# A two-layer graph network on one core: maxima with an operand in PSUM, a tile's own rows requested earlier, one slot and one loop test fewer, a square root in the last normalisation

## The chip, the cores and the metric

The kernel runs on one core of a Trainium2 chip. The core has five instruction queues that run side by side and meet through semaphores: TensorE (PE in the profile, its weight loads PEld), VectorE (DVE), ScalarE (ACT), GpSimd (POOL) and SyncE (SP), which issues DMAs. The metric is the device time of one execution in microseconds (us); the kernel before took 4130.41 us (median of 3 runs, 4128.99 to 4130.92).

## What is computed

12500 nodes with 64 features, 200000 edges sorted by destination, two layers. Cut to what matters:

```python
# layer 0
msg = relu(concat([x[dst], x[src], edge_attr, u[dst]]) @ W1 + b1)
agg = segment_sum(msg, dst)
x1  = layernorm(x + relu(concat([x, agg, u]) @ W2 + b2))
# layer 1, 8 relations
Z   = einsum('ni,rio->nro', x1, fc_weight)
e   = relu(sum(concat([Z[src, etype], Z[dst, etype]]) * attn[etype]))
m   = segment_max(e, dst)
a   = exp(e - m[dst]) / segment_sum(exp(e - m[dst]), dst)
out = layernorm(x1 + segment_sum(a * Z[src, etype], dst))
```

Destinations are skewed towards the low nodes (12500 times the square of a uniform number), so a node near the end has about 8 edges and one near the start far more.

## The kernel before

**Edges.** The edges are cut into runs of 512 (four chunks of 128), and two runs make a *group*: 196 groups (`NG`), the last with one run. All destinations of a run lie in a window of 96 nodes; here every run needs one window. A group's source rows are gathered by an indirect DMA per chunk, eight per group, issued by POOL (`gather`, L303; the instruction is L305): in layer 0 from `b_tab`, in layer 1 from `z_tab`, which layer 0 writes.

**Layer 0** (`sum0`, L331): the group's rows of `a_tab`, edge features and relative destinations are loaded by SP, POOL gathers, TensorE forms the messages, VectorE adds, ScalarE clips, TensorE sums by a one-hot matrix `oh` (made at L299 from a row of numbers that lies in PSUM, `psc`), and VectorE adds the sum into `xa`.

**Layer 1** (`sum1`, L527): the same shape of work, with a running maximum. The edge scores `e` are completed at L563 (which needs the gathered rows `zg`) and L564. Then L568 multiplies the one-hot matrix by the scores (128 partitions x 768 elements), and L571 takes the maximum over a run's four chunks in two halvings (384, then 192 elements). TensorE transposes the result (L577), VectorE reduces it (L582), and the maxima, exponentials (L615 to L619) and weighted sums (L623) follow, up to L627 and L628.

**Nodes.** 100 tiles of 125 nodes. A tile can be finished as soon as no later group adds to it. Which tile comes when is worked out from the destinations ahead of layer 0 (L241 to L264): from group 90 (`FIRST`) on there is one *slot* behind each group, and one more behind the last (`LATE`), 107 in all. A slot with nothing new to do repeats a tile; here the one behind the last group is such a slot. `finish0` (L374) loads the tile's own rows of `x` (L382), applies W2, normalises, and writes `x1_tab`, `z_tab` and `d_tab` (L400, L417, L421). `finish1` (L631) loads the tile's rows of `x1_tab` (L638), divides and adds; `scale1` (L652) normalises up to four tiles together and stores them (L670).

**Order.** Inside each layer the order of instructions on every engine is written out by hand. `sum0`, `sum1`, `finish0` and `finish1` are generators, cut by `yield`; each pass of the loop over `i` advances the pieces of groups `i+3` to `i-2` and of some slots. Loads are issued three groups ahead. Buffers are counted per tile (`zg` has five, `bg` and `dw` four).

**Behind each layer** stand loops that a graph with wider runs would need: over further windows (`each_window`, L281) and over tiles left (L515, L742). With these inputs all of them run zero times, but each loop is a test that all engines pass together after the transfers under way have landed.

Of the kernel before, what the change touches and what calls it, by code (L numbers as in the profile page):

```python
# [26 lines left out]
F32 = mybir.dt.float32  # L27
BF16 = mybir.dt.bfloat16
I32 = mybir.dt.int32
# [7 lines left out]
P = 125  # L37
# [14 lines left out]
FIRST = 90  # L52
LATE = 1
NS = NG + LATE
NSL = NS - FIRST
NQ1 = 4
# [6 lines left out]
def gnn_kernel(ctx: ExitStack, tc, x, xT, src, dstp, dst, et, eaT, u, W1, b1, W2, b2, fc, aw, out):  # L63
# [42 lines left out]
    nc.vector.memset(ones_row, 1.0)  # L106
    psc = fixed.tile([128, 512], F32, name="psc")
    nc.vector.tensor_copy(psc[:, :128], iota)
    iota_n, iota_r = psc[:EC, :W], psc[:EC, :NR]
# [31 lines left out]
    count_row = keep.tile([1, NRUN], I32, name="count_row")  # L141
    runs_more = keep.tile([1, 1], I32, name="runs_more")
    slot_row = keep.tile([1, NSL + 1], I32, name="slot_row")

# [23 lines left out]
    with (  # L168
# [71 lines left out]

        lo = [pre.tile([1, 2 * NS], F32, name=f"lo{i}") for i in range(2)]  # L241
        for t in lo:
            nc.vector.memset(t, float(N))
        nc.vector.tensor_reduce(lo[0][:, :NG - 1], both[:, 2, S:].rearrange("o (g s) -> o g s", s=S), AX.X, OP.min)
        step = 1
        while step < NS:
            nc.vector.tensor_tensor(lo[1][:, :NS], lo[0][:, :NS], lo[0][:, step:step + NS], OP.min)
            lo.reverse()
            step *= 2
# [3 lines left out]
        for t in up:  # L253
            nc.vector.memset(t, float(P))
        nc.vector.scalar_tensor_tensor(up[0][:, NSL:], lo[0][:, FIRST:NS], one, paces, OP.mult, OP.subtract)
        step = 1
# [5 lines left out]
        nc.vector.scalar_tensor_tensor(done, up[0][:, NSL:], float(P), paces, OP.min, OP.add)  # L262
        nc.vector.tensor_copy(slot_row[:, NSL:], done[:, NSL - 1:])
        nc.vector.tensor_scalar(slot_row[:, :NSL], done, -float(P), 0.0, OP.add, OP.max)  # L264
        nc.sync.dma_start(base_b, bases[0].partition_broadcast(EC))
# [14 lines left out]

    def each_window(body):  # L281

        last = nc.values_load(runs_more[0:1, 0:1], min_val=0, max_val=NRUN)
        with tc.For_i(0, last) as r:
            n = nc.values_load(count_row[0:1, ds(r, 1)], min_val=1, max_val=NWIN)
            with tc.For_i(1, n) as w:
                body(r, w)

# [85 lines left out]
    def finish0(work, psum, n0_of, dq):  # L374

        n0 = n0_of(ENG.DVE)
        yield
        xs = work.tile([2 * D, P], F32, name="xs")
        nc.vector.tensor_copy(xs, xa[:, ds(n0, P)])
        n0 = n0_of(ENG.SP)  # L380
        xn = work.tile([P, D], F32, name="xn")
        nc.sync.dma_start(xn, x[ds(n0, P), :])  # L382
        yield
# [15 lines left out]
        nc.vector.tensor_scalar(x1, y, mv[:, 0:1], v, OP.subtract, OP.mult)  # L399
        nc.sync.dma_start(x1_tab[ds(n0, P), :], x1)  # L400
        yield
# [15 lines left out]
        nc.sync.dma_start(  # L417
            z_tab[ds(n0 * NR, P * NR), :].rearrange("(p r) c -> p (r c)", r=NR),
            z.rearrange("p r c -> p (r c)"))
        parts(work, pw[:, NR:2 * NR], lambda i: dq[:, i * NR:(i + 1) * NR], [P, NR])  # L420
        nc.sync.dma_start(d_tab[ds(n0, P), :], dq)  # L421

# [36 lines left out]
    def group(g):  # L459
        if 0 <= g < NG:  # L460
            next(groups[g], None)

    def node(i):
        if i in slots:
            next(slots[i], None)

    with (
        tc.tile_pool(name="l0", bufs=2) as work,
        tc.tile_pool(name="l0_ps", bufs=1, space=PSUM) as pool,
        tc.manual_schedule(),  # L470
    ):
        psum = Banks(pool, {"po": "small", "pw": "small"})
        for i in range(-3, NS + 2):
            g = i + 3
            if g < NG:
                n, chunks, c = span(g)
                groups[g] = sum0(work, psum, n, chunks, src_i[:, c], rel[:, c], row_load(work, g),
                                 eaT[g * S:g * S + n], wins_load(g), aws[g % 4])
            if FIRST <= i < NS:
                slots[i] = finish0(work, psum, slot(i), dqs[i % 2])  # L480
            group(i + 3)
            node(i - 2)
            group(i)
            node(i - 1)
            node(i - 2)
            group(i)
            group(i + 2)
            group(i)
            node(i)
            node(i - 1)  # L490
            node(i - 2)
            node(i - 1)
            group(i)
            node(i)
            node(i - 1)
            group(i + 3)
            group(i + 1)
            node(i)

    with (  # L500
# [6 lines left out]

        each_window(more0)

    with (  # L510
        tc.tile_pool(name="r0n", bufs=1) as work,
        tc.tile_pool(name="r0n_ps", bufs=1, space=PSUM) as psum,
    ):
        begin = nc.values_load(slot_row[0:1, NSL:], min_val=0, max_val=N)
        with tc.For_i(begin, N, P) as n0:  # L515
            at = nc.s_assert_within(n0, 0, N - P, skip_runtime_bounds_check_because="the first node of a tile")
            all_of(finish0(work, psum, lambda engine: at, dqs[0]))
    nodes.close()
# [8 lines left out]
    def sum1(work, psum, n, chunks, idx, rel_of, et_of, row_of, wins_of):  # L527
# [38 lines left out]

        oe = work.tile([EC, n, KS, W], F32, name="oe")
        nc.vector.tensor_mul(oe.rearrange("p s i w -> p (s i) w"), oh, e.unsqueeze(2).to_broadcast([EC, n * KS, W]))  # L568
        half = KS // 2
        while half:  # L570
            nc.vector.tensor_max(oe[:, :, :half, :], oe[:, :, :half, :], oe[:, :, half:2 * half, :])  # L571
            half //= 2
        pt = psum.tile([128, n * (EC + W)], F32, name="pt")
        tt = pt[:W, :n * EC].rearrange("p (s e) -> p s e", s=n)
        rows = pt[:C, n * EC:].rearrange("p (s w) -> p s w", s=n)
        for s in range(n):
            nc.tensor.transpose(tt[:, s, :], oe[:, s, 0, :], ident[:EC, :EC])  # L577
        yield
# [51 lines left out]

    def finish1(work, psum, n0_of, y, mv):  # L631

        n0 = n0_of(ENG.Activation)
        own = work.tile([C, P], F32, name="own")
        nc.scalar.copy(own, acc[:, ds(n0, P)])
        n0 = n0_of(ENG.SP)
        xn = work.tile([P, D], F32, name="xn1")
        nc.sync.dma_start(xn, x1_tab[ds(n0, P), :])  # L638
        yield
        pl = psum.tile([P, C], F32, name="pl")  # L640
        nc.tensor.transpose(pl, own, ident[:C, :C])
        yield
        den = work.tile([P, 1], F32, name="den")

# [7 lines left out]
    def scale1(work, n0s_of, y, mv):  # L652
        n = len(n0s_of)

        v = work.tile([P, 2, n], F32, name="ln_v")
        nc.scalar.activation(v[:, 1, :], mv[:, :n, 1], AF.Ln, bias=eps)  # L656
        nc.scalar.activation(v[:, 0, :], v[:, 1, :], AF.Exp, scale=-0.5)
        yield
        nc.vector.tensor_mul(v[:, 1, :], v[:, 0, :], v[:, 0, :])
        again = work.tile([P, n], F32, name="ln_again")  # L660
        nc.vector.scalar_tensor_tensor(again, mv[:, :n, 1], EPS, v[:, 1, :], OP.add, OP.mult)
        nc.vector.tensor_scalar(again, again, -0.5, 1.5, OP.mult, OP.add)
        v = v[:, 0, :]
        nc.vector.tensor_mul(v, v, again)
        shift = work.tile([P, n], F32, name="ln_shift")
# [6 lines left out]
    with (  # L672
# [6 lines left out]

        for i in range(-3, NS + 4):  # L680
            g = i + 3
            if g < NG:
                n, chunks, c = span(g)
                groups[g] = sum1(work, psum, n, chunks, row_i[:, c], rel[:, c], et_i[:, c],
                                 row_load(work, g), wins_load(g))
            q, at = divmod(i - 2 - FIRST, NQ1)
            if FIRST <= i - 2 < NS:
                if at == 0:
                    ys[q] = (work.tile([P, NQ1, D], F32, name="y1"),
                             work.tile([P, NQ1, nc.vector.BN_AGGR_DIM], F32, name="ln_mv"))  # L690
                y, mv = ys[q]
                slots[i - 2] = finish1(work, psum, slot(i - 2), y[:, at, :], mv[:, at, :])
            group(i + 3)
            group(i)
            group(i - 1)
# [22 lines left out]
            q, at = divmod(i - 3 - FIRST, NQ1)  # L718
            if FIRST <= i - 3 < NS and (at == NQ1 - 1 or i - 3 == NS - 1):
                scales = {q: scale1(work, [slot(j) for j in range(i - 3 - at, i - 2)], *ys[q])}  # L720
                next(scales[q])

    with (
# [10 lines left out]

        each_window(more1)

    with (
        tc.tile_pool(name="r1n", bufs=1) as work,
        tc.tile_pool(name="r1n_ps", bufs=1, space=PSUM) as psum,
    ):  # L740
        begin = nc.values_load(slot_row[0:1, NSL:], min_val=0, max_val=N)
        with tc.For_i(begin, N, P) as n0:  # L742
            at = nc.s_assert_within(n0, 0, N - P, skip_runtime_bounds_check_because="the first node of a tile")
            y = work.tile([P, 1, D], F32, name="y1")
            mv = work.tile([P, 1, nc.vector.BN_AGGR_DIM], F32, name="ln_mv")
            all_of(finish1(work, psum, lambda engine: at, y[:, 0, :], mv[:, 0, :]))
            all_of(scale1(work, [lambda engine: at], y, mv))


# [40 lines left out]
```

## Time and profile before

| | |
|---|---|
| median of 3 runs | 4130.41 us |
| the profiled execution | 4140.92 us, span 4139.1 us, TensorE clock granted 0.572 |
| busy share of the span | PE 72%, PEld 56%, DVE 58%, ACT 35%, POOL 72% |
| first to last gather of layer 0 | 111.87 to 2062.87 us |
| first to last gather of layer 1 | 2104.23 to 4093.27 us |

The span runs from the first to the last instruction of the program; the execution's own time is 1.8 us longer. The profiled execution is 10.5 us above the median of the runs. The profile's page gives busy time by engine, the span in 40 slices, and groups of instructions by line: how many, mean ns of one, and what ended the idle time ahead of them. A line such as "x1563 | 1474.9, 944 | 575.2" is 1563 instructions, 1474.9 us busy, 944 ns each, 575.2 us idle ahead of them. In a timeline the columns are start, duration, engine, line, operation, output and inputs with their shapes, and in brackets the idle time before it and its releaser.

### The profile page before, as it was taken

Reading aid. Unit: us, or ns where it says so; the run is one execution under the profiler, and the core shown is the slowest. Engines: PE = TensorE matmul, PEld = TensorE weight load, DVE = VectorE, ACT = ScalarE, POOL = GpSimd, SP = SyncE. Lnnn points to the kernel's source line nnn. Section 1 sums busy time; section 2 is a strip of 40 time slices with the busy share of each in tenths; the row PEclk is TensorE's granted clock in tenths of the full one; section 3 lists DMA queues with packets and bytes.
Section 4 is the critical chain, followed back from the end, with each engine's and each line's share of the span. In section 5 each row is a group of like instructions: output and inputs, shape, how many; then the busy total and the mean of one; then the engine's idle time right before and its main releaser. Section 6 shows DMA issues by size and latency. Waiting matters only on the chain. (4 is left out here: it accounts for less than half of the span.)

```text
span 4139.1 us, 63111 instructions
## 1 busy us (share of the span) xinstructions
PE 3000.7 (72%) x16309; PEld 2329.7 (56%) x16310; DVE 2409.7 (58%) x7823; ACT 1434.5 (35%) x3697; POOL 3000.2 (72%) x3141
## 2 busy tenths in 40 slices
PE   4666766676999999999946665666666667666664
PEld 4455655565777767777735444454444555544553
DVE  3333333333555555555547666666677777777776
ACT  0000000000111111111155555555556666666665
POOL 1677777777777777777757777777777777777774
PEclk9655555555555565555555556655566555566655
DMA  5222222222333333333311111111112222212221
GB/s 131 53 45 46 45 45 46 45 46 44 74 80 78 77 80 79 78 80 77 72 34 28 29 28 28 29 28 28 28 30 35 35 35 34 36 34 35 35 35 24
DMA packets 317468, 201.76 MB, mean 49 GB/s; under 512 B 239840, under 2 KB 239970, under 8 KB 316746
## 3 DMA queue, kind: packets, MB, share of 16 engines
q0 software_dynamic: 100032, 103.43, 14.5%
q1 hardware_dynamic: 201819, 88.13, 9.1%
q10 hardware_dynamic: 15249, 6.10, 0.6%
q8 instruction: 132, 2.16, 0.2%
q14 instruction: 236, 1.93, 0.2%
HBM read 155.21 MB, written 42.17 MB: 48 GB/s over the span
## 5 line engine op out<-in xcount | busy, mean ns | idle before, releaser
L305 POOL DMA_INDIRECT bg<-b_tab,src_i x1563 | 1474.9, 944 | 575.2 <-issue 443.8
L305 POOL DMA_INDIRECT zg<-z_tab,row_i x1563 | 1512.9, 968 | 517.3 <-issue 396.3
L357 PE MATMUL pa<-oh,msg 128*64 128x96 f32 x3128 | 536.4, 363 | 282.7 <-ACT msg L352 281.9
L352 ACT ACTIVATE msg<-msg 128x512 f32<-128x512 f32 x196 | 123.2, 629 | 1706.8 <-DVE msg L351 1690.2
L347 PEld LDWEIGHTS pm<-aw,cb 128*128 128x128 f32 x3128 | 609.6, 299 | 140.3 <-issue 139.5
L357 PEld LDWEIGHTS pa<-oh,msg 128*64 128x64 f32 x3128 | 479.8, 221 | 303.9 <-ACT msg L352 299.3
L347 PE MATMUL pm<-aw,cb 128*128 128x64 f32 x3128 | 643.8, 391 | 0.0
L623 PE MATMUL pb<-oh,wz 128*65 128x96 f32 x3128 | 548.4, 367 | 16.0 <-ACT wz L619 2.9
L351 DVE TENSOR_TENSOR msg<-pm,bg 128x512 f32<-128x512 f32 x196 | 135.2, 690 | 694.0 <-DMA bg<-b_tab,src_i 580.1
L623 PEld LDWEIGHTS pb<-oh,wz 128*65 128x65 f32 x3128 | 494.3, 227 | 72.8 <-ACT wz L619 72.8
L619 ACT ACTIVATE wz<-zg,wz 128x64 f32<-128x64 f32 x1564 | 394.7, 335 | 6.4
L299 DVE TENSOR_TENSOR oh<-psc,rel 128x768 f32<-128x768 f32 x392 | 370.6, 945 | 9.3 <-DMA d_tab<-dq 6.5
L540 PE MATMUL ps_row<-row,ones_row 1*96 1x512 bf16 x391 | 208.0, 532 | 211.0 <-ACT off L541 200.1
L541 ACT ACTIVATE off<-ps_row,minus_p 96x512 bf16<-96x512 f32 x391 | 266.1, 681 | 263.7 <-PE ps_row L540 263.6
L577 PE MATMUL pt<-ident,oe 128*96 128x128 f32 x391 | 123.0, 417 | 323.0 <-DVE mq L369 323.0
L363 DVE TENSOR_TENSOR xa<-xa,pa 64x96 f32 x391 | 100.9, 258 | 334.7 <-PE pa L357 327.3
L584 PE MATMUL pt<-ident,m 96*65 96x96 f32 x782 | 176.5, 379 | 159.1 <-DVE m L582 159.1
L577 PEld LDWEIGHTS pt<-ident,oe 128*96 128x96 f32 x391 | 50.8, 184 | 416.2 <-issue 392.7
L342 DVE TENSOR_SCALAR cb<-ps_row,iota_p 96x1024 f32<-96x1024 f32 x196 | 246.2, 1256 | 8.8 <-PE ps_row L293 8.8
L584 PEld LDWEIGHTS pt<-ident,m 96*65 96x65 f32 x782 | 119.5, 220 | 176.1 <-DVE m L582 176.1
L293 PE MATMUL ps_row<-row,ones_row 1*96 1x512 bf16 x391 | 199.7, 609 | 17.8 <-DMA row<-rel_tab 16.4
L544 ACT ACTIVATE ohT<-off 96x1024 bf16<-96x1024 bf16 x196 | 206.7, 1054 | 6.3
(139 smaller groups left out, 3581.0 us busy)
## 6 DMA issues: line engine op xcount, KB each, us to landing
z_tab<-z SPq DMA_DIRECT2D x107, 253.9 KB
bg<-b_tab,src_i POOLq DMA_INDIRECT x1563
zg<-z_tab,row_i POOLq DMA_INDIRECT x1563
cb<-in_eaT SPq DMA_DIRECT2D x195, 128.0 KB
aw<-a_tab SPq DMA_DIRECT2D x391, 24.0 KB
dw<-d_tab SPq DMA_DIRECT2D x391, 4.7 KB
row<-rel_tab SPq DMA_DIRECT2D x390, 2.0 KB
xn<-in_x SPq DMA_DIRECT2D x107, 31.2 KB
```

The source lines that it names most:

```text
L293: nc.tensor.matmul(ps[:, s, :RE], ones_row, row[:, s, :], start=True, stop=True)
L299: nc.vector.tensor_tensor(oh, iota_n[:, None, :].to_broadcast([EC, n * KS, W]), rel_of.unsqueeze(2).to_broadcast([EC, n * KS, W]), OP.is_e ...
L305: nc.gpsimd.indirect_dma_start(out=to[:, k, :], out_offset=None, in_=table[:, :], in_offset=bass.IndirectOffsetOnAxis(ap=idx[:, k:k + 1], ...
L342: nc.vector.tensor_scalar(cb[:W, :, :], ps_row, iota_p[:W], None, OP.is_equal)
L347: nc.tensor.matmul(pm[:, k, :], cb[:, s, i * EC:(i + 1) * EC], aw_t[:, s, :], start=True, stop=True)
L357: nc.tensor.matmul(pa[D:, s, :], msg[:, k, :], oh[:, k, :], start=(i == 0), stop=(i == KS - 1))
L540: nc.tensor.matmul(ps_row[:, :RE], ones_row, row[:, s, :], start=True, stop=True)
L541: nc.scalar.activation(off[:, s, :], ps_row[:, :RE], AF.Abs, bias=minus_p[:W])
L544: nc.scalar.activation(ohT, off, AF.Relu, bias=1.0, scale=-1.0)
L584: nc.tensor.matmul(rows[:, s, :], m[:, s:s + 1].to_broadcast([W, C]), ident[:W, :W], start=True, stop=True)
L619: nc.scalar.activation(wz[:, k, :D], zg[:, k, :D], AF.Copy, scale=wz[:, k, D:])
L623: nc.tensor.matmul(sums[:, s, :], wz[:, k, :], oh[:, k, :], start=(i == 0), stop=(i == KS - 1))
```

## The change

- `LATE` goes: no slot behind the last group, 106 slots.
- `finish0` and `finish1` request the tile's own rows in a step of their own, first of all: in layer 0 with the loads of the slot's group, three passes earlier (six buffers); in layer 1 two passes earlier than before (five buffers).
- In `sum1` the product of one-hot matrix and scores is made in two halves, one in SBUF and one in the unused part of the PSUM tile `psc`; three maxima take the place of two, and each has one operand in PSUM.
- Behind each layer one outer loop, run once if tiles are left and not at all otherwise, holds both loops of before.
- `scale1` takes ScalarE's square root and VectorE's reciprocal in place of logarithm, exponential and a Newton step, and calls the exponential on one element behind it.

```diff
-LATE = 1
-NS = NG + LATE
-NSL = NS - FIRST
+NSL = NG - FIRST
...
+        nc.vector.tensor_scalar(rest, done[:, NSL - 1:], float(N), None, OP.is_lt)
...
-    def each_window(body):
-
-        last = nc.values_load(runs_more[0:1, 0:1], min_val=0, max_val=NRUN)
-        with tc.For_i(0, last) as r:
-            n = nc.values_load(count_row[0:1, ds(r, 1)], min_val=1, max_val=NWIN)
-            with tc.For_i(1, n) as w:
-                body(r, w)
+    def leftover(edges, node):
+
+        some = nc.values_load(rest[0:1, 0:1], min_val=0, max_val=1)
+        with tc.For_i(0, some):
+            last = nc.values_load(runs_more[0:1, 0:1], min_val=0, max_val=NRUN)
+            with tc.For_i(0, last) as r:
+                n = nc.values_load(count_row[0:1, ds(r, 1)], min_val=1, max_val=NWIN)
+                with tc.For_i(1, n) as w:
+                    edges(r, w)
+            begin = nc.values_load(slot_row[0:1, NSL:], min_val=0, max_val=N)
+            with tc.For_i(begin, N, P) as n0:
+                node(nc.s_assert_within(n0, 0, N - P, skip_runtime_bounds_check_because="the first node of a tile"))
...
     def finish0(work, psum, n0_of, dq):
 
+        at = n0_of(ENG.SP)
+        xn = work.tile([P, D], F32, name="xn", bufs=6)
+        nc.sync.dma_start(xn, x[ds(at, P), :])
+        yield
         n0 = n0_of(ENG.DVE)
         yield
         xs = work.tile([2 * D, P], F32, name="xs")
         nc.vector.tensor_copy(xs, xa[:, ds(n0, P)])
-        n0 = n0_of(ENG.SP)
-        xn = work.tile([P, D], F32, name="xn")
-        nc.sync.dma_start(xn, x[ds(n0, P), :])
         yield
...
-        for i in range(-3, NS + 2):
+        for i in range(-3, NG + 2):
...
-            if FIRST <= i < NS:
-                slots[i] = finish0(work, psum, slot(i), dqs[i % 2])
+            if FIRST <= g < NG:
+                slots[g] = finish0(work, psum, slot(g), dqs[g % 2])
             group(i + 3)
+            node(i + 3)
             node(i - 2)
...
-        oe = work.tile([EC, n, KS, W], F32, name="oe")
-        nc.vector.tensor_mul(oe.rearrange("p s i w -> p (s i) w"), oh, e.unsqueeze(2).to_broadcast([EC, n * KS, W]))
         half = KS // 2
-        while half:
-            nc.vector.tensor_max(oe[:, :, :half, :], oe[:, :, :half, :], oe[:, :, half:2 * half, :])
-            half //= 2
+        by_run, es = oh.rearrange("p (s i) w -> p s i w", s=n), e.rearrange("p (s i) -> p s i", s=n)
+        oe = work.tile([EC, n, half, W], F32, name="oe")
+        other = psc[:EC, 128:128 + n * half * W].rearrange("p (s i w) -> p s i w", s=n, i=half)
+        for to, i in ((oe, slice(0, half)), (other, slice(half, KS))):
+            nc.vector.tensor_mul(to, by_run[:, :, i, :], es[:, :, i].unsqueeze(3).to_broadcast([EC, n, half, W]))
+        t = work.tile([EC, n, W], F32, name="t")
+        nc.vector.tensor_max(other[:, :, 1, :], oe[:, :, 1, :], other[:, :, 1, :])
+        nc.vector.tensor_max(t, oe[:, :, 0, :], other[:, :, 0, :])
+        nc.vector.tensor_max(t, t, other[:, :, 1, :])
...
-    def finish1(work, psum, n0_of, y, mv):
-
+    def finish1(work, psum, n0_of, y_of):
+
+        n0 = n0_of(ENG.SP)
+        xn = work.tile([P, D], F32, name="xn1", bufs=5)
+        nc.sync.dma_start(xn, x1_tab[ds(n0, P), :])
+        yield
         n0 = n0_of(ENG.Activation)
         own = work.tile([C, P], F32, name="own")
         nc.scalar.copy(own, acc[:, ds(n0, P)])
-        n0 = n0_of(ENG.SP)
-        xn = work.tile([P, D], F32, name="xn1")
-        nc.sync.dma_start(xn, x1_tab[ds(n0, P), :])
         yield
...
-        v = work.tile([P, 2, n], F32, name="ln_v")
-        nc.scalar.activation(v[:, 1, :], mv[:, :n, 1], AF.Ln, bias=eps)
-        nc.scalar.activation(v[:, 0, :], v[:, 1, :], AF.Exp, scale=-0.5)
-        yield
-        nc.vector.tensor_mul(v[:, 1, :], v[:, 0, :], v[:, 0, :])
-        again = work.tile([P, n], F32, name="ln_again")
-        nc.vector.scalar_tensor_tensor(again, mv[:, :n, 1], EPS, v[:, 1, :], OP.add, OP.mult)
-        nc.vector.tensor_scalar(again, again, -0.5, 1.5, OP.mult, OP.add)
-        v = v[:, 0, :]
-        nc.vector.tensor_mul(v, v, again)
+        v = work.tile([P, n], F32, name="ln_v")
+        nc.scalar.activation(v, mv[:, :n, 1], AF.Sqrt, bias=eps)
+        back = work.tile([1, 1], F32, name="back")
+        nc.scalar.activation(back, none[:1], AF.Exp)
+        yield
+        nc.vector.reciprocal(v, v)
...
             group(i + 3)
+            node(i)
             group(i)
```

More of the change, by code (lines that the diff above doesn't have):

```diff
@@ L142, in gnn_kernel @@
     runs_more = keep.tile([1, 1], I32, name="runs_more")
+    rest = keep.tile([1, 1], I32, name="rest")
     slot_row = keep.tile([1, NSL + 1], I32, name="slot_row")
@@ L237, in gnn_kernel @@
         nc.vector.tensor_copy(runs_more, more)
-        lo = [pre.tile([1, 2 * NS], F32, name=f"lo{i}") for i in range(2)]
+        lo = [pre.tile([1, 2 * NG], F32, name=f"lo{i}") for i in range(2)]
         for t in lo:
@@ L245, in gnn_kernel @@
         step = 1
-        while step < NS:
-            nc.vector.tensor_tensor(lo[1][:, :NS], lo[0][:, :NS], lo[0][:, step:step + NS], OP.min)
+        while step < NG:
+            nc.vector.tensor_tensor(lo[1][:, :NG], lo[0][:, :NG], lo[0][:, step:step + NG], OP.min)
             lo.reverse()
@@ L254, in gnn_kernel @@
             nc.vector.memset(t, float(P))
-        nc.vector.scalar_tensor_tensor(up[0][:, NSL:], lo[0][:, FIRST:NS], one, paces, OP.mult, OP.subtract)
+        nc.vector.scalar_tensor_tensor(up[0][:, NSL:], lo[0][:, FIRST:NG], one, paces, OP.mult, OP.subtract)
         step = 1
@@ L399, in finish0 @@
         nc.vector.tensor_scalar(x1, y, mv[:, 0:1], v, OP.subtract, OP.mult)
-        nc.sync.dma_start(x1_tab[ds(n0, P), :], x1)
+        nc.sync.dma_start(x1_tab[ds(at, P), :], x1)
         yield
@@ L417, in finish0 @@
         nc.sync.dma_start(
-            z_tab[ds(n0 * NR, P * NR), :].rearrange("(p r) c -> p (r c)", r=NR),
+            z_tab[ds(at * NR, P * NR), :].rearrange("(p r) c -> p (r c)", r=NR),
             z.rearrange("p r c -> p (r c)"))
         parts(work, pw[:, NR:2 * NR], lambda i: dq[:, i * NR:(i + 1) * NR], [P, NR])
-        nc.sync.dma_start(d_tab[ds(n0, P), :], dq)
+        nc.sync.dma_start(d_tab[ds(at, P), :], dq)
     def slot(i):
@@ L506, in more0 @@
             all_of(sum0(work, psum, 1, KS, idx, rl, lambda: row, eaT[ds(r, 1)], lambda engine: [base], aws[0]))
[L508 to L517, printed above, removed]
+        leftover(more0, lambda at: all_of(finish0(work, psum, lambda engine: at, dqs[0])))
     nodes.close()
@@ L576, in sum1 @@
         for s in range(n):
-            nc.tensor.transpose(tt[:, s, :], oe[:, s, 0, :], ident[:EC, :EC])
+            nc.tensor.transpose(tt[:, s, :], t[:, s, :], ident[:EC, :EC])
         yield
@@ L642, in finish1 @@
         yield
+        y, mv = y_of()
         den = work.tile([P, 1], F32, name="den")
@@ L678, in gnn_kernel, with y_of @@
         groups, slots, ys, scales = {}, {}, {}, {}
-        for i in range(-3, NS + 4):
+        def y_of(i):
+            q, at = divmod(i - FIRST, NQ1)
+            if at == 0:
+                ys[q] = (work.tile([P, NQ1, D], F32, name="y1"),
+                         work.tile([P, NQ1, nc.vector.BN_AGGR_DIM], F32, name="ln_mv"))
+            return ys[q][0][:, at, :], ys[q][1][:, at, :]
+        for i in range(-3, NG + 4):
             g = i + 3
@@ L685, in gnn_kernel @@
                                  row_load(work, g), wins_load(g))
[L686 to L692, printed above, removed]
+            if FIRST <= i < NG:
+                slots[i] = finish1(work, psum, slot(i), lambda i=i: y_of(i))
             group(i + 3)
+            node(i)
             group(i)
@@ L718, in gnn_kernel @@
             q, at = divmod(i - 3 - FIRST, NQ1)
-            if FIRST <= i - 3 < NS and (at == NQ1 - 1 or i - 3 == NS - 1):
+            if FIRST <= i - 3 < NG and (at == NQ1 - 1 or i - 3 == NG - 1):
                 scales = {q: scale1(work, [slot(j) for j in range(i - 3 - at, i - 2)], *ys[q])}
@@ L733, in more1, with node1 @@
             all_of(sum1(work, psum, 1, KS, idx, rl, etx, lambda: row, lambda engine: [base]))
[L735 to L743, printed above, removed]
+        def node1(at):
             y = work.tile([P, 1, D], F32, name="y1")
             mv = work.tile([P, 1, nc.vector.BN_AGGR_DIM], F32, name="ln_mv")
-            all_of(finish1(work, psum, lambda engine: at, y[:, 0, :], mv[:, 0, :]))
+            all_of(finish1(work, psum, lambda engine: at, lambda: (y[:, 0, :], mv[:, 0, :])))
             all_of(scale1(work, [lambda engine: at], y, mv))
+        leftover(more1, node1)
 def kernel(x, src, dst, edge_attr_32, edge_type_8, L0_gnn_u, L0_gnn_W1, L0_gnn_b1, L0_gnn_W2,
```

## The prediction

> **What bounds the kernel now.** I read the page's busy table, then its groups by line, then which engine waited for what, then the timeline of POOL and VectorE side by side, and last the timeline where one layer ends and the next begins.
>
> No engine is over 72% busy on the page, yet one paces both layers. POOL issues 1563 gathers per layer, one after the other:
>
> ```profile
> L305 POOL DMA_INDIRECT bg<-b_tab,src_i x1563 | 1474.9, 944 | 575.2 <-issue 443.8
> L305 POOL DMA_INDIRECT zg<-z_tab,row_i x1563 | 1512.9, 968 | 517.3 <-issue 396.3
> ```
>
> Between two gathers lie 0.30 us of issue, never over 0.32 within a layer. Layer 0's gathers run from 111.87 to 2062.87 us and layer 1's from 2104.23 to 4093.27 us, so the span is 111.9 (preparation) + 1951.0 + 41.4 (seam) + 1989.0 + 45.8 (tail) = 4139.1. TensorE at "9" in the second half of layer 0, VectorE at "7" in layer 1 and every queue wait of SP lie beside POOL's chain. Only two kinds of thing move the end: the time of a gather, and the seam and tail, where POOL has nothing to do.
>
> The two rows differ by 24 ns per gather, 1563 x 0.024 = 37.5 us. In layer 1 every group of eight has seven gathers of 944 ns and one long one. The timeline shows its neighbour:
>
> ```profile
> 3001.28 0.17 DVE L563 TENSOR_TENSOR e<-e,zg 128x8 f32<-128x8 f32 x1 [1.42 <-DMA zg<-z_tab,row_i]
> 3001.68 0.96 DVE L568 TENSOR_TENSOR oe<-oh,e 128x768 f32<-128x768 f32 x1
> 3002.68 0.95 DVE L571 TENSOR_TENSOR oe<-oe 128x384 f32<-128x384 f32 x2
> ```
> ```profile
> 3001.11 0.94 POOL L305 DMA_INDIRECT zg<-z_tab,row_i  x1 [0.30 <-issue]
> 3002.36 1.09 POOL L305 DMA_INDIRECT zg<-z_tab,row_i  x1 [0.30 <-issue]
> 3003.76 0.95 POOL L305 DMA_INDIRECT zg<-z_tab,row_i  x1 [0.30 <-DVE mq L369]
> ```
>
> Over all groups the excess of the long gather is the end of one VectorE instruction, counted from the gather's start, less 127 ns: here L568 ends at 3002.64, 0.28 behind the start, and the excess is 0.15. A gather whose start falls at least 50 ns behind the start of L568 and more than 127 ns ahead of its end is held; one whose start lies anywhere else is not. So a gather needs something for a moment at its start that L568 keeps. Replayed for all groups this gives 37.2 us, the records 37.4. 183 of the 195 long gathers overlap L568 and the replay puts six down to the maxima (L571): the held gather gets through in the 34 ns and the start-up between L568 and L571. L299 of the same size (947 ns, one operand in PSUM) overlaps 380 gathers and lengthens none. The phase is steady because L563 waits for the landing of the group's own last gather: in half the groups L568 starts 593 to 700 ns ahead of the gather that it holds.
>
> The seam's end and the tail's:
>
> ```profile
> 2077.47 0.22 DVE L388 TENSOR_TENSOR y<-po,c 125x64 f32<-125x64 f32 x1 [0.50 <-PE po L385]
> 2078.95 0.33 SPq L382 DMA_DIRECT2D xn<-in_x  x1
> 2081.49 0.22 DVE L389 SCALAR_TENSOR_TENSOR y<-y,xn 125x64 f32<-125x64 f32 x1 [3.79 <-DMA xn<-in_x]
> ...
> 2090.53 0.26 SPq L417 DMA_DIRECT2D z_tab<-z  x1
> ...
> 2095.47 0.26 SPq L421 DMA_DIRECT2D d_tab<-dq  x1
> ...
> 2104.23 0.95 POOL L305 DMA_INDIRECT zg<-z_tab,row_i  x1 [41.17 <-DVE er L555]
> ...
> 4120.37 0.33 SPq L638 DMA_DIRECT2D xn<-x_tab  x1
> 4122.34 0.28 DVE L647 SCALAR_TENSOR_TENSOR y<-pl,den,xn 125x64 f32<-125x64 f32 x1 [6.29 <-DMA xn<-x_tab]
> ```
>
> Slot 195's own rows are requested late and VectorE stands 3.79 us; then slot 196 follows; then two loop tests. In the tail the request of slot 196's rows stands behind four output stores.
>
> **The change: maxima.** The multiply becomes two of 128x384 (558 ns, the one L568 row of that size), both with both inputs in SBUF, the second written to PSUM. They don't depend on each other, and independent neighbours start 80 ns before the predecessor's end (L571 to L369 above), so the second runs from 477 to 1034 ns behind the first's start. The maxima, three of 128x192 (358 ns, L571's row of that size), each have a PSUM operand: like L299 they hold nothing. That relieves those six, 1.3 us. VectorE's work per group goes from 957+34+559+34+358 = 1942 ns to about 2100, and the waits at L563 (mean 1.5 us) hide that; without them L563 would be late by 0.15 us a group, moving the phase.
>
> What matters is the held gather. L568 ended 957 ns behind its start; the second half ends at 1034. The other 184 are held 77 ns longer, 184 x 0.077 = +14.2 us; groups whose multiply starts less than 527 ns ahead of the gather now escape or fall to the shorter first half. Replayed group by group: 43.1 us, +6.
>
> [...] L568's mean is 958 ns and a gather never delays it by more than some 70 ns. [...] by the rows the sum is +6. [...]
>
> No row shows two SBUF inputs with a PSUM output. From below: it holds nothing, only the first half does, and the replay leaves 1.7 us (-36). From above: it holds as L568 and also starts later. I take "holds", as the nearest row is L568, with the same two inputs.
>
> **Seam.** Own rows early: slot 194's wait at L389 (1.22 us) and slot 195's (3.79) go. What is late next is TensorE: z's matmuls of slot 194 end about 2078.4, then the transposition of slot 195 and x1T near 2079.5 instead of 2083.91. From there z takes as long as slot 196's did (x1T 2090.64, z store 2094.96, d_tab store 2095.47), and its store waits for the previous one's landing, so the last z store goes out near 2083.9 instead of 2094.96: -11.1, slot 196's whole step included. Slot 196 only repeats the last tile: worked out from the destinations, the slots up to 195 already reach node 12500, so the loop behind them stays empty. One loop test less: POOL passed the first at 2100.5 and the second at 2102.6: -2.1. Seam -13.2.
>
> **Tail.** VectorE's longer multiply and maxima delay the last two groups by 0.3. The square root leaves two table loads (1.28 us each) per four tiles as before, and two VectorE instructions instead of five (-0.6). The four stores end near 4118.9; they go at 1.74 us each, so those of slots 194 and 195 go near 4120.6 and 4122.4, where the last went at 4130.1: -7.7. The rows of slot 195 have long landed. One test less, SP 4132.0 to 4133.7: -1.9, less rounding. Tail -9.6.
>
> **At nothing.** The requests moved ahead (a register load of 1.7 us and one DMA per slot) pass on SP behind the group's own loads and ahead of stores; SP waits some 700 us in each layer for buffers and loads run three groups ahead, so POOL, which waits only for its own buffers (five), sees nothing. Without that cover each would cost up to 2 us of 10.3 a group. With six and five buffers no request waits for a tile in use. The "rest" instruction, 0.19 us, is hidden behind loads.
>
> Sum on the profiled execution: -13.2 - 9.6 + 6 = -16.8, from its own time of 4140.9 (span 4139.1) to 4124. The median of the runs is 4130.4, 10.5 below the profiled one; the difference carries over: 4113.6, say 4114.
>
> **Rivals.** *PSUM output frees the gather* (0.14): -22.8 - 36 gives 4071. For it: the gap that L299 leaves; against: L299's freedom is that of an input. *Phase* (0.16): if the second half starts 34 ns behind the first's end, as dependent pairs do, and 50 ns later besides, the gather slips through between them in two of three groups: 20 us left, 4130.4 - 22.8 - 17 = 4091. *Slower* (0.06): L563 released some 120 ns later against the gathers, so that the second half starts just ahead of each one's need: held 380 ns, 195 x 0.38 = 74 us, +37 - 23, 4144. It decides from 351 ns a group, where the holds reach 68.4 us and outweigh seam and tail by 0.2%; the seam's savings don't touch it. *It doesn't do what it says* (0.06): the seam waits for stores of z that land no earlier; only the tail's half comes, 4130.4 - 9.6 + 6 = 4127.
>
> **Numbers.** My case has 0.58, with 4100 to 4124 of its own (seam and tail 3 each way, phase). The measurement can tell 0.2%, 8.3 us. Faster: my case, the first two rivals and a little less at the edges, 0.84; same 0.09; slower 0.07. The range takes in the PSUM rival: 4068 to 4124.
>
> **What would show it.** zg's mean gather of 971 ns against 968, one long gather per group of about 1.2 us ending with the second multiply; 945 would mean that PSUM output frees it. First gather of layer 1 about 28 us behind layer 0's last (41.4 before); tail near 36 (45.8). No wait of L389 for xn. Wrong if POOL shows gaps over 0.31 us inside a layer.

## The result, and the profile after

The changed kernel took 4107.67 us (median of 6 runs, 4105.61 to 4110.41), the kernel before 4130.85 us beside it: a ratio of 0.9944, 95% interval 0.9931 to 0.9957, which is 23 us less. The forecast was 4114, 17 us less. The profiled execution of the changed kernel took 4110.41 us, its span 4108.6.

The page of the changed kernel, the gathers of both layers (the columns are as before; the lines of the code have moved, L305 to L311):

```profile
L311 POOL DMA_INDIRECT bg<-b_tab,src_i x1563 | 1475.2, 944 | 574.6 <-issue 435.2
L311 POOL DMA_INDIRECT zg<-z_tab,row_i x1563 | 1507.6, 965 | 501.4 <-issue 423.1
```

POOL still paces both layers, 0.30 us between gathers throughout. But zg's mean is 965 ns, where 971 was expected: the long gathers add up to 32.1 us, less than before (37.4) instead of more. Cut at the first and last gather of each layer, in us:

| | preparation | layer 0 | seam | layer 1 | tail | span |
|---|---|---|---|---|---|---|
| before | 111.9 | 1951.0 | 41.4 | 1989.0 | 45.8 | 4139.1 |
| after | 111.3 | 1951.3 | 25.5 | 1983.7 | 36.9 | 4108.6 |
| forecast | 111.9 | 1951.0 | 28.2 | 1995 | 36.2 | 4122 |

The timelines of VectorE and of POOL around one group of layer 1 in the changed kernel:

```profile
3003.35 0.56 DVE L571 TENSOR_TENSOR oe<-oh,e 128x384 f32<-128x384 f32 x1
3003.83 0.56 DVE L571 TENSOR_TENSOR psc<-oh,e 128x384 f32<-128x384 f32 x1
3004.42 0.36 DVE L573 TENSOR_TENSOR psc<-oe,psc 128x192 f32<-128x192 f32 x1
```
```profile
3002.83 0.94 POOL L311 DMA_INDIRECT zg<-z_tab,row_i  x1 [0.30 <-issue]
3004.08 1.11 POOL L311 DMA_INDIRECT zg<-z_tab,row_i  x1 [0.30 <-DMA zg<-z_tab,row_i]
3005.50 0.94 POOL L311 DMA_INDIRECT zg<-z_tab,row_i  x1 [0.31 <-issue]
```

The two multiplies start 0.48 us apart, as forecast from a neighbour in the kernel before that starts 0.08 us ahead of the end of L571 (3003.63):

```profile
3003.55 0.15 DVE L369 CAST mq<-pb 96x2 bf16<-96x2 f32 x1
```

The second multiply, into PSUM, is the one that runs when the gather at 3004.08 starts. It ends 0.31 us behind that start, and the gather is 0.17 us too long: the end less about 130 ns, the same law that L568 showed before (less 127 ns).

The seam and the tail of the changed kernel, from its timeline:

```profile
2071.86 0.22 DVE L395 TENSOR_TENSOR y<-po,c 125x64 f32<-125x64 f32 x1 [0.27 <-PE po L392]
2072.12 0.22 DVE L396 SCALAR_TENSOR_TENSOR y<-y,xn 125x64 f32<-125x64 f32 x1
...
2079.71 0.26 SPq L424 DMA_DIRECT2D z_tab<-z  x1
2080.21 0.26 SPq L428 DMA_DIRECT2D d_tab<-dq  x1
2085.31 0.23 SPq L444 DMA_DIRECT2D row<-rel_tab  x1
...
2088.06 0.95 POOL L311 DMA_INDIRECT zg<-z_tab,row_i  x1 [25.32 <-issue]
...
4092.08 9.21 SPq L670 DMA_DIRECT2D out<-y  x6
```

L396, which is L389 of before, no longer waits for xn. The last store of z goes out at 2079.71, and six output stores in a row end the work, where four, a request and three more did before.

### The profile page after: what moved, and what is told of

It is laid out like the page before. It is cut to its first block, busy times and chain, and to the rows that moved or that the text cites. A ratio compares the mean times of both kernels' runs of the same rounds, so it can differ in the third digit from the quotient of the medians.

```text
span 4108.6 us, 63192 instructions
## 1 busy us (share of the span) xinstructions
PE 2993.0 (73%) x16301; PEld 2321.8 (57%) x16302; DVE 2440.2 (59%) x8117; ACT 1432.1 (35%) x3693; POOL 2995.2 (73%) x3141
## 5 line engine op out<-in xcount | busy, mean ns | idle before, releaser
L311 POOL DMA_INDIRECT bg<-b_tab,src_i x1563 | 1475.2, 944 | 574.6 <-issue 435.2
L311 POOL DMA_INDIRECT zg<-z_tab,row_i x1563 | 1507.6, 965 | 501.4 <-issue 423.1
L357 DVE TENSOR_TENSOR msg<-pm,bg 128x512 f32<-128x512 f32 x196 | 135.3, 690 | 698.9 <-DMA bg<-b_tab,src_i 553.7
L305 DVE TENSOR_TENSOR oh<-psc,rel 128x768 f32<-128x768 f32 x392 | 370.6, 945 | 12.3 <-DMA row<-rel_tab 9.5
L580 PE MATMUL pt<-ident,t 128*96 128x128 f32 x391 | 123.5, 419 | 326.6 <-DVE mq L375 326.3
L580 PEld LDWEIGHTS pt<-ident,t 128*96 128x96 f32 x391 | 50.8, 184 | 418.6 <-issue 395.1
L299 PE MATMUL ps_row<-row,ones_row 1*96 1x512 bf16 x391 | 197.8, 604 | 17.5 <-DMA row<-rel_tab 16.2
```

The source lines that it names most:

```text
L299: nc.tensor.matmul(ps[:, s, :RE], ones_row, row[:, s, :], start=True, stop=True)
L305: nc.vector.tensor_tensor(oh, iota_n[:, None, :].to_broadcast([EC, n * KS, W]), rel_of.unsqueeze(2).to_broadcast([EC, n * KS, W]), OP.is_e ...
L311: nc.gpsimd.indirect_dma_start(out=to[:, k, :], out_offset=None, in_=table[:, :], in_offset=bass.IndirectOffsetOnAxis(ap=idx[:, k:k + 1], ...
```

## The experiments

The theory, in keeping with L568 (two inputs in SBUF, 183 gathers held) and L299 (one input in PSUM, none held of 380 that overlap it): a gather of layer 1 is held by whichever VectorE instruction with both inputs in SBUF is running as it starts; it ends later by what is left of that instruction at its start, less about 130 ns. Which instruction that is follows from how soon gathered rows land. The gain is in seam and tail. The main rival: the maxima's own reads were the hold and PSUM has relieved them, as the shorter layer 1 suggests.

In what follows *message* is the last group's L351 (L357 in the changed kernel), and *hold* is the sum of what layer 1's gathers last over 944 ns. *Landing* is the time from the start of a group's last gather to the end of VectorE's wait for its rows, median over the early groups of layer 0, where the change alters nothing. Each ratio is to the kernel before, run on the same chip. The kernel before, the maxima alone, everything but the maxima and the multiply freed ran on one chip; the changed kernel, the multiply freed with the maxima in SBUF, the delay and the two loop tests on a second; the slot kept on a third; and three runs, told of last, on a fourth.

**The kernel before, once more**, for a profile beside the others.

> The kernel before, once more, for a profile on the chip of the other runs. Theory (a gather is held until the end of the multiply that runs at its start; how far that is depends on how soon the gathered rows land): if the rows of layer 0 land 2.50 us behind the start of a group's last gather, as in the changed kernel's profile, the long gathers of layer 1 add up to about 28 us and the span is near 4130; if they land at 2.57 us, as in the first profile, to 37 us and 4139. Rival (the landing has no part in it): 37 us whatever the landing.

Landing 2.55 us, hold 38.8, span 4138.9; median 4139.8, ratio 1.0004 (0.9996 to 1.0013). So the rows landed as late as in the first profile (2.57, hold 37.4), and the case of 2.50 us did not come up.

**The maxima alone.**

```diff
-        oe = work.tile([EC, n, KS, W], F32, name="oe")
-        nc.vector.tensor_mul(oe..., oh, e...)
-        while half: ...
+        (the two halves and three maxima of the change)
```

> The kernel before with the halved multiply and the PSUM maxima alone. Theory: the second half ends 77 ns later than the whole multiply did, so layer 1's holds grow by 4 to 6 us and the time with them: 4134 to 4137. Rival (the maxima's SBUF reads held the gathers, PSUM relieves them): layer 1 shorter by 5 us or more, 4126 or less.

Ratio 1.0011 (1.0004 to 1.0018), median 4143.0 against 4138.1: 5 us slower. Hold 41.7 against 38.8 for the kernel before on the same chip (landing 2.56 and 2.55), layer 1 1993.3 against 1990.3. The rival falls: the maxima as changed cost 3 us in layer 1; the tail, 47.1 against 45.7, has 1.4 more. (The two spans differ by 2.2 us only, because the last message came 2.9 us sooner in this profile.) The 3 us are not far from the spread of single profiles: the hold is 37.4, 38.8 and 39.1 in the three with the whole multiply, and 38.7 to 42.2 in four with the halves where the change puts them. That the maxima do not gain is shown by the time.

**Everything but the maxima.**

```diff
-        (the two halves and three maxima of the change)
+        (one multiply of 128x768 and two maxima in SBUF, as before)
```

> The changed kernel with the old multiply and the old maxima: seam, tail and square root alone. Theory: the whole gain is in the seam (15.9) and the tail (8.9): 4106 or a little less, 2 to 6 us faster than the changed kernel. Rival (the maxima gain 5 us): 4112 to 4113, 5 us slower than the changed kernel.

Ratio 0.9943 (0.9929 to 0.9956), median 4115.2. Seam 26.2, tail 36.3, hold 39.1. The time lay above the 4106 that was expected, and nearer the rival's 4112 to 4113, because this chip's kernel before takes 4138, not 4130; the ratio is that of the whole change (0.9944 at first, 0.9952 once more). The gain is in seam and tail, all of it.

**The changed kernel, once more.**

> The changed kernel, once more, for a profile on the chip of the other runs. Theory: hold in layer 1 about 32 us if layer 0's rows land at 2.50 us, about 42 us if they land at 2.55 to 2.57 us, as in the kernel with the maxima alone (41.7). Rival (the changed kernel itself makes rows land sooner): landing at 2.50 us again, while the kernel before on the same chip runs as in its first profile.

Ratio 0.9952 (0.9936 to 0.9969), median 4118.2 against 4139.1. Landing 2.55, hold 38.7, where about 42 was expected: zg's row is back at 969 ns.

```profile
L311 POOL DMA_INDIRECT zg<-z_tab,row_i x1563 | 1514.2, 969 | 500.2 <-issue 423.4 <-DMA zg<-z_tab,row_i 33.5 <-DVE t L574 18.6
```

So the changed kernel does not make rows land sooner. In its first profile rows landed at 2.50 us in layer 0 too, some 70 ns sooner than in the first profile of before, in code that the change leaves alone, and that moved the multiply from 3090 to 3027 ns behind the group's last gather. The trace's records of single DMA packets say the same: the last packet of a group's last gather ends 2.05 us behind the gather's start in that profile, and 2.10 to 2.13 in the ten others from chips of this kind. Within one chip the figure differs by 0.02 us at most (2.11 to 2.12 in four profiles, 2.10 to 2.12 in four), so this looks like a matter of the chip; the chips of the two first profiles are not on record. The lower hold of 32 goes with the earlier landing. A replay of that profile's gathers with the old, undivided multiply gives 28 us of hold, an estimate, so on equal terms the change cost a little there as well. No profile stands beside the runs of 4130; that they too had early landings is likely and not shown.

**The multiply freed.** The scores go to an unused strip of `psc`, so that neither multiply has two inputs in SBUF.

```diff
+        ep = psc[:EC, 96:96 + n * KS]
+        nc.vector.tensor_copy(ep, e)
...
-        by_run, es = ..., e.rearrange("p (s i) -> p s i", s=n)
+        by_run, es = ..., ep.rearrange("p (s i) -> p s i", s=n)
```

> The changed kernel with the scores copied to PSUM ahead of the two multiplies (one small VectorE copy more per group), so that no instruction of the multiply and the maxima reads two SBUF inputs. Theory: the long gathers vanish, their sum falls from 32 us to 2 at most, mean gather 945 ns, time near 4077. Rival (the maxima were the holders, already relieved, or the hold is not of the inputs): no change against the changed kernel, 4108.

Ratio 0.9854 (0.9839 to 0.9870), median 4078.6 against 4138.1: 59 us, more than twice the change. The long gathers are gone (eight are left, of 0.2 us together), and layer 1 takes 1951.1 us, as layer 0 does. The gathers of the page's two rows, then VectorE and POOL around one group:

```profile
L311 POOL DMA_INDIRECT bg<-b_tab,src_i x1563 | 1475.2, 944 | 575.1 <-issue 448.7 <-DMA row<-rel_tab 99.0 <-DMA bg<-b_tab,src_i 16.8
L311 POOL DMA_INDIRECT zg<-z_tab,row_i x1563 | 1475.0, 944 | 500.9 <-issue 421.0 <-DMA zg<-z_tab,row_i 30.8 <-ACT top L599 18.3
```
```profile
2978.95 0.17 DVE L567 COPY psc<-e 128x8 f32<-128x8 f32 x1
2979.16 0.55 DVE L573 TENSOR_TENSOR oe<-oh,psc 128x384 f32<-128x384 f32 x1
2979.74 0.56 DVE L573 TENSOR_TENSOR psc<-oh,psc 128x384 f32<-128x384 f32 x1
```
```profile
2979.43 0.94 POOL L311 DMA_INDIRECT zg<-z_tab,row_i  x1 [0.30 <-issue]
2980.68 0.94 POOL L311 DMA_INDIRECT zg<-z_tab,row_i  x1 [0.30 <-issue]
```

The gather at 2979.43 starts 0.27 us behind the start of the first multiply and 0.28 ahead of its end, and takes 0.94 us; all 183 gathers that stood so to L568 in the kernel before were held. 62 gathers of this profile start so far inside one of the multiplies (50 ns behind its start or more, over 140 ns ahead of its end); none takes over 0.95 us, where the law would give 8.5 us of hold, an estimate from their starts. The rest of the 39 us goes with the phase. The copy puts the first multiply 3.30 us behind the group's last gather instead of 3.09, and the two halves start 0.59 us apart instead of 0.48, so most gathers now start where nothing would hold them. This edit mixes the two; the next two experiments take them apart. The output in PSUM, which the changed kernel has too, frees nothing: there the multiply into PSUM holds 163 of 185 long gathers. VectorE does one instruction more per group, and the kernel is faster.

**The multiply freed, the maxima left in SBUF**, on the kernel before (`ep` in place of `e` in the multiply, nothing else).

> The kernel before with the scores copied to PSUM, the multiply whole, the old maxima with both operands in SBUF. Theory: the multiply no longer holds; the maxima still can, but they run 1.1 to 1.7 us behind the multiply's start and fall between two gathers' starts: holds of 0 to 2 us, 37 us faster than the kernel before (ratio 0.991). Rival (the maxima hold too once the multiply does not): 15 us or more of holds left, at most 22 us faster.

Ratio 0.9944 (0.9928 to 0.9961), 4115.9 against 4139.1. Hold 15.4, not 0 to 2, and 23 us faster: the expectation failed, and the rival's (15 us or more, at most 22 faster) held within 1 us. 155 gathers are held by the maxima, 145 of them by the second:

```profile
3010.09 0.95 DVE L570 TENSOR_TENSOR oe<-oh,psc 128x768 f32<-128x768 f32 x1
3011.08 0.95 DVE L573 TENSOR_TENSOR oe<-oe 128x384 f32<-128x384 f32 x2
```
```profile
3010.57 0.94 POOL L305 DMA_INDIRECT zg<-z_tab,row_i  x1 [0.30 <-DMA zg<-z_tab,row_i]
3011.82 1.03 POOL L305 DMA_INDIRECT zg<-z_tab,row_i  x1 [0.30 <-issue]
```

The gather at 3010.57 starts 0.48 us inside the freed multiply, 0.47 ahead of its end, and is not held. So do 187 gathers in all; none takes over 0.95 us, where the law would give an estimated 69 us of hold. That is the plain evidence that the hold is of the inputs: here the later phase would have made it longer. The next, at 3011.82, starts inside the maxima, which end at 3012.03, and is 0.09 long. The replay behind the expectation had taken that gather's start from the trace, where the hold that the edit removes had put it 0.2 us later, out of the maxima's reach. So an operand of the maxima in PSUM is worth some 15 us, but only once the multiply is freed: with both freed, 144 gathers start as far inside one of the maxima, and they take 944 ns in the mean.

**A delay.** One instruction that has no use but to take time goes ahead of the multiplies of the changed kernel.

```diff
+        late = work.tile([EC, 3, W], F32, name="late")
+        nc.vector.tensor_copy(late, iota_n[:, None, :].to_broadcast([EC, 3, W]))
```

> The changed kernel with one more VectorE instruction per group, a copy of 128x288 from PSUM ahead of the multiplies, which only delays them by about 0.26 us (0.45 us of work). Theory (the phase decides): the gather's start falls between the two halves, holds fall from 32 or 42 us to 9 to 15, and the kernel is 20 to 30 us faster than the changed one for doing more. Rival (VectorE's work counts): slower or the same; longer holds by 190 x 0.26 = 49 us if the end of the multiply alone counts.

Ratio 0.9888 (0.9871 to 0.9904), median 4091.8: 26 us faster than the changed kernel for 0.45 us more of VectorE's work in each group. Hold 11.4. Where the multiplies now stand to a gather:

```profile
3006.76 0.45 DVE L567 COPY late<-psc 128x288 f32<-128x288 f32 x1
3007.12 0.55 DVE L573 TENSOR_TENSOR oe<-oh,e 128x384 f32<-128x384 f32 x1
3007.59 0.56 DVE L573 TENSOR_TENSOR psc<-oh,e 128x384 f32<-128x384 f32 x1
```
```profile
3007.53 0.96 POOL L311 DMA_INDIRECT zg<-z_tab,row_i  x1 [0.30 <-DMA zg<-z_tab,row_i]
```

The gather starts just ahead of the end of the first half and of the start of the second, and is held 0.02 us. The phase decides, not the amount of work. The multiplies, with both inputs in SBUF, stand 0.25 us later against the gathers than in the changed kernel, nearly as in the kernel with the multiply freed: so of the 39 us that went there, an estimated 27 to 30 go by the phase alone, and 9 to 11 needed the inputs freed.

**Two loop tests** in the changed kernel.

```diff
-        with tc.For_i(0, some):
-            (both loops inside)
+        (both loops, one after the other)
```

> The changed kernel with the two loops behind each layer one after the other, as before, instead of one test. Theory: the first test stands in the time in which SP waits for the last stores to land, so the second costs 1 to 2 us in the seam and 1.4 to 1.9 us in the tail: 2.5 to 4 us slower. Rival (tests cost nothing at the end): the same time.

4120.2 against 4118.2, ratios 0.9954 (0.9937 to 0.9970) and 0.9952: not told apart by time. In the profiles the last store of z to the first gather of layer 1 takes 8.9 us against 7.4, and the last output store to the end 9.6 against 7.6: 3.4 us together. POOL passes the first of two tests 0.2 us behind SP's wait for the landings, and the second 2.2 us later. With a single test SP waits for the landings ahead of it, at its next load (L444; in the first profile the wait ends at 2085.27 us and POOL passes the test at 2087.17), so 1.9 of that test's time is no longer hidden. That is why one test fewer is worth less than one test.

**The slot kept.** The changed kernel with `LATE = 1` and `NS` in place of `NG` wherever slots are counted.

> The changed kernel with the slot behind the last group kept, its rows requested early, once more. Theory: on a chip whose gathered rows land within 3 us, as in the first runs, the seam grows from 24 to 26 us by one step of about 4 us to 28 to 30, the tail from 37 by about 2 us; 5 to 6 us slower than the changed kernel, ratio to the kernel before near 0.9965. Rival (the slot was the bulk of the gain, the early rows little): seam 33 us or more, 10 us slower.

Ratio 0.9957 (0.9940 to 0.9973), seam 29.1, tail 37.7; hold 42.2 with landing at 2.57. By time it is not told apart from the changed kernel (0.9952). The seam fits the theory: the last group's message to the last store of z takes 16.4 us, against 12.1 to 12.4 in the changed kernel and 23.2 to 24.6 in four profiles with both the slot and the late requests. The slot's step is 4 us; with the slot there, the early requests are worth 7.

Three earlier runs met a chip on which this could not be read:

> The changed kernel with the slot behind the last group kept (107 slots), its own rows requested early. Theory: in the seam the slot's step comes last again, one step of about 4 us (x1T to x1T without the wait for rows) and no more; in the tail a fifth and sixth store become a seventh, 1.7 us, and the own copy and the sums of one more tile lie in the stores' shadow: 5 to 6 us slower than the changed kernel. Rival (the slot was the bulk of the gain): 10 us or more slower.

> The changed kernel with a tile's own rows requested where they were before, the slot behind the last group gone. Theory: in the seam slots 194 and 195 wait 1 and 4 us for their rows again, 5 to 6 us slower; in the tail the rows of slot 195 are requested ahead of the four stores, so nothing: 5 to 6 us slower than the changed kernel in all, none of it inside the layers. Rival (the early request costs or gains inside the layers, on SP): the span between first and last gather of a layer differs by 3 us or more.

> The same kernel as the one before it, a second look at its profile. Theory: seam and tail within 2 us of the first look, with the TensorE clock in the seam explaining the rest. Rival (they vary by more, so that no part of a few us can be told from one profile).

There the kernel before took 5470 us; slot kept gave a ratio of 0.9995 (0.9986 to 1.0004), late requests 0.9988 (0.9980 to 0.9997), and the same kernel again, run once, 5453 us. In the median VectorE first read a group's rows 35 to 41 us behind its last gather instead of 2.6, so POOL waited for buffers and paced nothing:

```profile
3014.22 0.94 POOL L311 DMA_INDIRECT zg<-z_tab,row_i  x1 [0.30 <-issue]
3023.46 0.94 POOL L311 DMA_INDIRECT zg<-z_tab,row_i  x1 [8.30 <-ACT top L597]
```

The rows were not late: the last packet of a group's last gather ended 2.06 to 2.07 us behind the gather's start there, sooner than in the ten profiles above. The engines stood for something that the profile calls remote and doesn't name. The sum into `xa`, first in the changed kernel's second profile, then in that with late requests:

```profile
L369 DVE TENSOR_TENSOR xa<-xa,pa 64x96 f32 x391 | 100.8, 258 | 325.7 <-PE pa L363 317.9
L369 DVE TENSOR_TENSOR xa<-xa,pa 64x96 f32 x391 | 100.9, 258 | 771.5 <-remote 587.6
```

What made that chip slow stays open. Its seams of 51 to 55 us say nothing of the parts of 25, and the two profiles with late requests differ by 4 us in the seam. But the stretch from the last message to the last store of z was not drawn out: with the slot kept it is 16.4 us there too. With late requests and no slot it is 17.6 and 16.3, some 4 to 5.5 us more than in the changed kernel. That is all there is on the late requests alone; they were not undone on a chip of the first kind.

## Why the prediction was right, and where it was not

**POOL as the bound: right.** Layer 0 kept its 1951 us and no gap inside a layer exceeds 0.32 us in either profile. The sign of being wrong, a gap over 0.31, was set too close: the longest is 0.314 in the changed kernel and was 0.318 before. When the holds go, the kernel gets faster by just their sum: 39 us of hold less is 39 us of layer 1 less with the multiply freed (1990.3 to 1951.1 beside 38.8 to -0.5).

**What holds a gather: right.** The change's means missed the holder, as argued from L568's 183 gathers; the multiply into PSUM holds 163 of 185 long gathers in the changed kernel's second profile, 10 fall to the first half and 11 to a third instruction with two SBUF inputs (L596). L299 was weaker evidence than it looked: of the 380 gathers that overlap it in layer 1, only 8 start where the law would hold them. The changed kernel mends that: 188 start so inside the same instruction (L305 there), and none takes over 0.953 us. The nearest row (L568, two SBUF inputs) was the right stand-in for a form that the trace did not have, and the rival "PSUM output frees the gather" falls. That an instruction holds by its inputs was the author's assumption, which those two rows alone did not show; the runs do: 187 gathers start inside the freed multiply, and none takes over 0.95 us. The time of a hold is what the rows gave: what is left of the instruction at a gather's start, less about 130 ns.

**The size of the hold: the mis-sized term.** +6 was forecast; it is +2.9 for the maxima alone on one chip, and -0.1 for the whole change (38.8 to 38.7) between two profiles with equal landing. The sum's weak point was to take the phase of one execution for the kernel's. In the changed kernel, some 50 ns between landings go with 6.6 us of hold (32.1 and 38.7), as much as the term, and the first profile had the early one; that layer 1 came out 5.3 us shorter there was luck. The phase rival named this and looked for it in the spacing of the two halves; the halves were spaced as forecast (0.48 us), and it was the landing that moved. VectorE's work from the multiplies to the last maximum was put at about 2100 ns; it is 2207. The multiplies overlap, as taken (0.48 us from start to start, 0.56 long), but the maxima do not (0.38 to 0.40 us from start to start, 0.35 to 0.36 long), and the wait for rows hid it (1.40 us at L562 in the group shown).

**The seam: right in its steps.** Message to last z store was to shrink by 11.1 us; it went from 23.2 to 12.1 in the first pair of profiles. The test was put at 2.1; from the z store to the first gather the two pairs of profiles show 0.9 and 1.6 less. The 3.9 left of the seam's 15.9 are no part of the forecast: the last group's message came 8.9 us behind the last gather in the first profile of before and 4.8 to 7.7 in three others of that kind, 5.0 in the changed kernel's and 4.5 to 6.8 in five others with early requests. It varies from profile to profile, and why was not looked into. How the 11 divide depends on what is undone: the slot alone is worth 4, the early requests alone 4 to 5.5, both 11 to 12. About 3 are left over, near slot 196's own wait for its rows (3.35), which goes with either.

**The tail: right.** -9.6 was forecast, -9.0 measured: the last output store 29.2 us behind the last gather, against 36.8, and 7.6 us from there to the end, against 9.05, so the test is worth 1.4 and not 1.9 here; put back into the changed kernel it costs the 1.9. The square root was not undone by itself: its share, put at 0.6, is not shown.

**The sum.** -13.2 - 9.6 + 6 became, between the second profiles of both kernels (landing 2.55 in each), -16.9 in the seam (3.1 of it the earlier message), -8.9 in the tail, 0 in layer 1 and +1 in the preparation: -24.6 in the span, -21 in the medians. Between the first two profiles it was -30.5, and -23 in the medians. The 10.5 us by which the first profile lay above its runs did not carry over, as the sum had taken it to: the changed kernel's first profile lies 2.7 above its runs.

## What to carry to other kernels

When one queue of gathers paces a kernel, look at the spread of its durations first: here seven of eight gathers took 944 ns and one took longer, something else held that one, and the excess lined up against the other engine's instruction ends named the holder. Then free every input that held, in the order of what comes first, since freeing the second holder alone bought nothing here (ratio 1.0011). What freed the multiply here was an input in PSUM (187 gathers start inside it, none over 0.95 us); its output in PSUM did not (163 of 185 long gathers held), and splitting it only moved its end, from 0.96 to 1.04 us behind its start. The edit that frees it also moves it: before the gain is put down to the freeing, count the gathers that still start inside it.

## What was not expected of the hardware

- The time in which gathered rows land in code that no edit touched was 2.50 us in one profile and 2.55 to 2.57 in ten others, and the hold went with it: 32.1 and 38.7 us in two profiles of one kernel of 4110 us.
- On one chip the kernel took 5470 us, though its single gathers lasted 944 ns and their packets ended 2.06 to 2.07 us behind the start; what the engines stood for there is open.
- An added VectorE instruction of 0.45 us, 196 times over, made the kernel 26 us faster.
